# The last layer of a four-layer graph network: whole tiles instead of halves, and a written order

## The chip, the cores and the metric

The kernel runs on one core of one Trainium2 chip. The core has a matrix engine (TensorE, PE in the profile; PEld is its weight load), a vector engine (VectorE, DVE), an activation engine (ScalarE, ACT), GpSimd (POOL) and SyncE (SP), which issues most of the transfers here. Each engine works through its own list of instructions in order and waits on semaphores for the others. Matrix results land in PSUM, eight banks of 512 float32 columns on 128 partitions; everything else is in SBUF. The metric is the device time of one execution in microseconds (us). PSUM is small, and which operations touch it decides how wide they can be in this kernel.

## The reference

Four layers over a graph of 4096 nodes with 64 features; each adds its result to `x` and normalises the rows. The change is in the last one, which works on the Poincare ball:

```python
def _logmap(x, y, c):
    sub = _mobius_add(-x, y, c)
    sub_norm = jnp.maximum(jnp.linalg.norm(sub, axis=-1, keepdims=True), MIN_NORM)
    ...
    arg = jnp.clip(sqrt_c * sub_norm, 0.0, TANH_CLIP)
    return 2.0 / (sqrt_c * lam_x) * jnp.arctanh(arg) * sub / sub_norm
...
deg = jnp.maximum(adj.sum(axis=1, keepdims=True), 1e-08)
w = adj / deg
log_ij = _logmap(x[:, None, :], x[None, :, :], c)
agg = jnp.einsum('ij,ijc->ic', w, log_ij)
transformed = agg @ weight + bias
return _expmap(origin, transformed, c)
```

For every pair of nodes (i, j) a factor is needed that depends on both rows and is the same for (i, j) and (j, i), up to what belongs to one row alone. The kernel computes a number v per pair by a matrix product, then the factor min(ln(v + root), T_MAX) / root, where root is the square root of a floored `v*v - 1` (in scaled units). It multiplies the adjacency by the factor and sums over j with another matrix product. What belongs to one row is multiplied in afterwards.

## The kernel before

The 4096 nodes form 8 groups of 512 (`GW`), in the order of the list `seq`. A tile is a pair of groups (i, j) with j at or after i in that order: 36 tiles, 8 of them on the diagonal. They are taken row by row: row 0 has 8 tiles, row 1 has 7, and so on; the first tile of a row is the diagonal one. A tile is 128 partitions x 4 blocks x 512 columns, that is 2048 columns. Because the factor is symmetric, an off-diagonal tile serves twice: its own adjacency tile (`own`, L1463) is multiplied by the factor, and the mirrored one (`mirrored`, L1469) by the factor turned (transposed) on PE.

The steps of a tile, with halves of two blocks (1024 columns) as the unit n:

- `product` (L1484): PE writes v into a pair of PSUM banks, `ps_v` with two such pairs.
- `square` (L1498): ACT squares v into `w`; `opposite` (L1505): PE adds a small correction product onto the same v.
- `less_one` (L1518): DVE subtracts the one and floors it, in SBUF.
- ACT: Ln of `w` in place (L1718), Exp with scale 0.5 into `rt`, the root (L1719), later Exp with scale -0.5 in place, one over the root (L1745).
- DVE `plus root` (L1743): `rt` becomes v + root; this reads v from PSUM and so frees the bank pair for the `product` of half n + 2.
- ACT: Ln of `rt` (L1754).
- DVE `factor` (L1728): the smaller of `rt` and T_MAX, times `w`, into `f`; then `own products` (L1731): adjacency times `f`.
- `turn` (L1523): PE transposes blocks of `f`, four at a time into one PSUM bank of `ps_p` (two banks, used in turn); DVE multiplies each bank into the mirrored adjacency (L1541), 512 columns per instruction. A diagonal tile turns only one quarter (L1532, L1534), and its second half has only 256 columns per block.
- `gather` (L1544): PE sums the weighted adjacency times the node features into a bank of `ps_a` (two banks): partitions 0 to 63 for row i (L1555), partitions 64 to 127 for the mirrored sum of the tile before (L1567), which in later rows starts from the sum carried in `tb` (L1563). ACT copies the sums to `tb` (L1574, L1578).

One turn of the loop does one half: factor and own products lie two halves behind the roots, the gather one more, the transposes one or two more. PE's matrix products of `product`, `opposite` and `gather` are held in the order of the program by `in_order`; the transposes and all of DVE's and ACT's instructions are ordered by the planner of the language, which places each by priority when its inputs are due. All the tile's steps use the same pools of buffers: four halves of `w`, three of `rt`, two tiles of `f`, three tiles of each adjacency.

Besides the tiles there are small steps in the list `seam`, one taken per turn: the end of the layer before (normalisation of its last groups), the preparation `weights` and `factors`, and for each finished row the five steps of `finals` (L1631), on tiles of at most 128 x 512, with their PSUM results in `ps_p` as well. `right(i)` (L1443) prepares the right-hand sides for a row: two products into `ps_p`, each copied by ACT (L1451). SP issues the loads of 1 MB each, three tiles ahead at the start and then as buffers come free. After the loop the rest of `seam` is worked off: that is the tail in which the last two groups are finished.

The change replaces the loop and the functions around it; `right`, `factors`, `weights`, `finals` and everything ahead of the last layer stay.

Of the kernel before, what the change touches and what calls it, by code (L numbers as in the profile page):

```python
# [62 lines left out]
def gnn4_kernel(  # L63
# [28 lines left out]
    CB = 4  # L92
# [1333 lines left out]
    with tc.tile_pool(name="o3", bufs=1) as op, tc.tile_pool(name="cols3", bufs=3) as cols_p, tc.tile_pool(  # L1426
        name="w3", bufs=4
    ) as wp3, tc.tile_pool(name="el3", bufs=3) as el, tc.tile_pool(name="f3", bufs=2) as fp, tc.tile_pool(
        name="r3", bufs=2
    ) as rp, tc.tile_pool(name="ps_v3", bufs=2, space=PSUM) as ps_v, tc.tile_pool(  # L1430
        name="ps_a3", bufs=2, space=PSUM
    ) as ps_a, tc.tile_pool(name="ps_p3", bufs=2, space=PSUM) as ps_p:
        HB = CB // 2

# [40 lines left out]
        def columns(n):  # L1475

            i, j = tiles[n // 2]
            return slice(2 * P if i == j and n % 2 else 0, GW)

        rights, sums, fs = {}, {}, {}  # L1480
        vs, ws, rts = {}, {}, {}
        NU = 2 * NT

        def product(n):  # L1484

            if n >= NU:
                return
            i, j = tiles[n // 2]
            vs[n] = ps_v.tile([P, HB, GW], F32, name="v_ps")
            cs = columns(n)  # L1490
            for k in range(HB):
                jb = j * CB + (n % 2) * HB + k
                half = slice(jb % 2 * F, jb % 2 * F + F)
                in_order(nc.tensor.matmul(  # L1494
                    vs[n][:, k, cs], lhsT=tr_c[half, jb // 2, :], rhs=rights[i][0][half, cs], start=True, stop=True
                ))

        def square(n):  # L1498
            if n >= NU:
                return  # L1500
            ws[n] = wp3.tile([P, HB, GW], F32, name="w3")
            cs = columns(n)
            nc.scalar.activation(ws[n][:, :, cs], vs[n][:, :, cs], AF.Square)  # L1503

        def opposite(n):  # L1505
            if n >= NU:
                return
            i, j = tiles[n // 2]
            cs = columns(n)
            for k in range(HB):  # L1510
                jb = j * CB + (n % 2) * HB + k
                half = slice(jb % 2 * F, jb % 2 * F + F)
                in_order(nc.tensor.matmul(
                    vs[n][:, k, cs], lhsT=tr_o[half, jb // 2, :], rhs=rights[i][1][half, cs],
                    start=False, stop=True, skip_group_check=True,
                ))

        def less_one(n):  # L1518
            if n < NU:
                w = ws[n][:, :, columns(n)]  # L1520
                nc.vector.tensor_scalar(w, w, -SCALE * SCALE, V_FLOOR * (V_FLOOR + 2.0) * SCALE**2, ALU.add, ALU.max)  # L1521

        def turn(n):  # L1523

            t, h = n
            i, j = tiles[t]
            work = []
            if i == j:
                tp = ps_p.tile([P, GW], F32, name="post", tag="post")
                for k in range(HB):  # L1530
                    for b in range(HB):
                        nc.tensor.transpose(tp[:, cols(HB * k + b)], fs[t][:, b, cols(HB + k)], ident)  # L1532
                to = own[t][:, HB:CB, 0 : HB * P]
                work.append(lambda: nc.vector.tensor_tensor(to, tp.rearrange("p (k i) -> p k i", k=HB), to, ALU.mult))  # L1534
                return work
            for b in (HB * h, HB * h + 1):
                tp = ps_p.tile([P, GW], F32, name="post", tag="post")
                for k in range(CB):
                    nc.tensor.transpose(tp[:, cols(k)], fs[t][:, k, cols(b)], ident)  # L1539
                to = mirrored[t][:, b, :]  # L1540
                work.append(lambda to=to, tp=tp: nc.vector.tensor_tensor(to, tp, to, ALU.mult))  # L1541
            return work

        def gather(t, h, tm):  # L1544

            if t is not None:
                i, j = tiles[t]
                if i == j and h == 0:
                    sums[i] = ps_a.tile([P, GW], F32, name="sums_ps")
                bank = sums[i]  # L1550
            else:
                bank = sums[seq[-1]]
            for k in (HB * h, HB * h + 1):
                if t is not None:
                    in_order(nc.tensor.matmul(  # L1555
                        bank[0:F, :], lhsT=nat_c[:, j * CB + k, :], rhs=own[t][:, k, :],
                        start=(i == j and k == 0), stop=(j == seq[-1] and k == CB - 1), skip_group_check=True,
                    ))
                if tm is not None:
                    above, below = tiles[tm]  # L1560
                    if k == 0 and above != seq[0]:

                        in_order(nc.tensor.matmul(  # L1563
# [3 lines left out]
                    in_order(nc.tensor.matmul(  # L1567
# [3 lines left out]
            work = []  # L1571
            if tm is not None and h:
                to = tb[F:P, gcols(tiles[tm][1])]
                work.append(lambda: nc.scalar.copy(to, bank[F:P, :]))  # L1574
            if t is not None and h and tiles[t][1] == seq[-1]:
                g = tiles[t][0]
                copy = nc.vector.tensor_copy if g == seq[-1] else nc.scalar.copy
                work.append(lambda: copy(tb[0:F, gcols(g)], bank[0:F, :]))  # L1578
                seam.extend(finals(g))
            return work  # L1580
# [113 lines left out]
        turns, late_turns, gathers = {}, {}, {}  # L1694

        for t in range(3):
# [117 lines left out]
```

## Time and profile before

| | us |
|---|---|
| median of three runs | 1417.04 |
| lowest, highest | 1411.5, 1420.06 |
| the profiled execution, its own time | 1415.59 |
| its span, first to last instruction | 1413.9 |
| busy in the span: PE, DVE, ACT | 1308.5, 1052.1, 803.7 |
| first `plus root` (L1743) of the last layer starts at | 982.7 |
| L1743 that opens the last tile starts at | 1375.7 |

The times of steps come from the profiled execution. In a row of groups the columns are the line and the engine, what is written from what, the shape, the count, then the busy time of the group and the mean in nanoseconds of one, then the idle time of the engine just ahead of them and what ended it. A row of the timeline gives start and duration in us. A row of windows gives, for a stretch of time, its length, then busy time and number of instructions of PE, PEld, DVE, ACT and POOL, the clock granted to PE (1.00 is full), the share of the DMA engines and GB/s. Successive instructions of one engine overlap a little, so the step from start to start can be shorter than the duration.

### The profile page before, as it was taken

To read this page: it belongs to the slowest core of one execution; us is meant where nothing else is said; L and a number is where in the kernel's file an instruction comes from. 1 tells how busy PE (TensorE), PEld (TensorE's weight loads), DVE (VectorE), ACT (ScalarE), POOL (GpSimd) and SP (SyncE) were. 2 spreads that over 40 slices of the span, in tenths; PEclk is the share of its full clock that TensorE was granted. 3 is DMA by queue.
4 is the path that set the end of the run, shared out by engine and by line. 5 is a ranking of instruction groups with operands and counts; after the bars stand their busy time and mean duration, and the time that the engine had idled before them with its cause. 6 is when DMAs were issued, how large, how long until landed. Compare 5 with 4: busy or idle time off the path is not lost.

```text
span 1413.9 us, 18980 instructions
## 1 busy us (share of the span) xinstructions
PE 1308.5 (93%) x6766; PEld 604.3 (43%) x6766; DVE 1052.1 (74%) x2012; ACT 803.7 (57%) x1339; POOL 109.8 (8%) x191
## 2 busy tenths in 40 slices
PE   7999999999899998999999999998888899989893
PEld 5655555565344333444444333333333333333331
DVE  6799999898343266788885123446999999999986
ACT  5544443443000115654423675744989999999993
POOL 2110111110122000000110000000000000000000
PEclk9999999999999999999998999998899999999997
DMA  9999999999699999999985555444245454445420
GB/s 326 408 412 411 397 411 409 409 396 398 230 365 388 380 421 378 377 345 331 329 310 191 186 185 179 146 154 175 66 177 189 148 232 150 182 155 202 154 97 12
DMA packets 108191, 382.16 MB, mean 270 GB/s; under 512 B 20276, under 2 KB 20280, under 8 KB 76472
## 3 DMA queue, kind: packets, MB, share of 16 engines
q1 hardware_dynamic: 87096, 296.17, 57.1%
q0 software_dynamic: 12736, 76.29, 13.1%
q10 hardware_dynamic: 8256, 8.39, 1.7%
q8 instruction: 56, 0.92, 0.3%
q14 instruction: 47, 0.39, 0.1%
HBM read 294.05 MB, written 85.20 MB: 268 GB/s over the span
## 4 chain that ended last, share of the span: by engine, by line
PE 59%; ACT 17%; DVE 15%; DMA 4%; issue 3%; ACTq 0%; DVEq 0%; SPq 0%
PE a_ps L1111 8%; PE pass L566 7%; PE w_ps L566 5%; PE tp L657 5%; PE p_ps L1102 5%; PE pass L559 5%; PE cnt_ps L1373 4%; PE acc_ps L1333 4%; DMA raw<-in_adj_dram 3%; ACT w L1718 3%; ACT rt L1719 3%; ACT w L1503 3%; DVE lows L690 2%; ACT rt L1754 2%; DVE dpart L688 2%
## 5 line engine op out<-in xcount | busy, mean ns | idle before, releaser
L664 ACT COPY at<-tp 128x512 f32<-128x512 f32 x248 | 127.8, 598 | 120.8 <-issue 91.1
L1378 ACT ACTIVATE wt<-cnt_ps 128x512 uint16<-128x512 f32 x208 | 115.5, 595 | 72.6 <-PE cnt_ps L1373 67.9
L688 DVE TENSOR_REDUCE dpart<-raw 128x4 f32<-128x2048 f32 x64 | 145.5, 2275 | 5.5 <-DMA raw<-in_adj_dram 5.3
L1555 PE MATMUL sums_ps<-at_d,some 128*64 128x512 f32 x288 | 146.5, 629 | 2.7 <-DVE at_d L1534 1.7
L690 DVE TENSOR_REDUCE lows<-raw 128x1 f32<-128x2048 f32 x64 | 145.5, 2274 | 0.0
L657 PE MATMUL tp<-ident,raw 128*128 128x128 f32 x1024 | 130.8, 281 | 10.1 <-DMA raw<-in_adj_dram 9.0
L657 PEld LDWEIGHTS tp<-ident,raw 128*128 128x128 f32 x1024 | 114.7, 143 | 47.2 <-issue 36.3
L1111 PE MATMUL a_ps<-at,nat_a 128*64 128x512 f32 x512 | 123.3, 609 | 0.0
L1567 PE MATMUL sums_ps<-at_m,some 128*64 128x512 f32 x224 | 110.2, 615 | 0.0
L1494 PE MATMUL v_ps<-rv,tr_a 64*128 64x512 f32 (+1 forms) x288 | 81.7, 645 | 23.2 <-DVE rt L1743 23.2
L566 PE MATMUL pass<-at,cheb_n 128*128 128x512 f32 x224 | 99.2, 601 | 2.4 <-DVE cheb_n L588 1.9
L566 PE MATMUL w_ps<-at,cheb_n 128*128 128x512 f32 x208 | 93.5, 593 | 0.0
L1743 DVE SCALAR_TENSOR_TENSOR rt<-v_ps,rt 128x1024 f32<-128x1024 f32 x72 | 83.5, 1161 | 4.2 <-ACT rt L1719 3.6
L1373 PE MATMUL cnt_ps<-m,follow 128*64 128x512 fp8e4 x480 | 81.7, 391 | 4.6 <-ACT wt L1378 1.5
L1728 DVE SCALAR_TENSOR_TENSOR f<-rt,w 128x1024 f32<-128x1024 f32 x72 | 83.6, 1163 | 1.1 <-ACT rt L1754 1.0
L1731 DVE TENSOR_TENSOR at_d<-at_d,f 128x1024 f32<-128x1024 f32 x72 | 83.7, 1162 | 0.1
L1541 DVE TENSOR_TENSOR at_m<-post,at_m 128x512 f32<-128x512 f32 x112 | 75.4, 686 | 9.5 <-PE post L1539 9.2
L1380 DVE TENSOR_SCALAR wt<-cnt_ps 128x512 uint16<-128x512 f32 x48 | 33.2, 692 | 63.1 <-PE cnt_ps L1373 60.4
L1754 ACT ACTIVATE rt<-rt 128x1024 f32<-128x1024 f32 x72 | 72.1, 1005 | 7.8 <-DVE rt L1743 7.4
L1718 ACT ACTIVATE w<-w 128x1024 f32<-128x1024 f32 x72 | 71.9, 1000 | 5.0 <-DVE w L1521 5.0
L1539 PE MATMUL post<-ident,f 128*128 128x128 f32 x448 | 69.0, 284 | 5.4 <-DVE at_m L1541 4.3
L1745 ACT ACTIVATE w<-w 128x1024 f32<-128x1024 f32 x72 | 72.4, 1006 | 0.6
(396 smaller groups left out, 2222.7 us busy)
## 6 DMA issues: line engine op xcount, KB each, us to landing
at<-adj_t SPq DMA_DIRECT2D x119, 1024.0 KB, 7.9
raw<-in_adj_dram SPq DMA_DIRECT2D x64, 1024.0 KB, 13.5
adj_t<-at POOLq DMA_DIRECT2D x62, 1024.0 KB, 8.1
at_d<-adj_t SPq DMA_DIRECT2D x36, 1024.0 KB, 4.8
at_m<-adj_t SPq DMA_DIRECT2D x28, 1024.0 KB, 6.9
m<-mask_t SPq DMA_DIRECT2D x120, 128.0 KB, 2.8
m<-mask_t SPq DMA_DIRECT2D x60, 256.0 KB, 4.1
mask_t<-mask ACTq DMA_DIRECT2D x28, 256.0 KB, 7.9
```

Of the source, the lines that this page charges most:

```text
L566: in_order(nc.tensor.matmul(ps, lhsT=cheb_n[:, jb, k : k + 2, :], rhs=rhs, start=first, stop=last))
L657: in_order(nc.tensor.transpose(tp[:, cols(b)], raw[:, b, cols(k)], ident))
L664: nc.scalar.copy(at[:, k, :], tp)
L688: in_order(nc.vector.tensor_reduce(dpart[:, g, c, :], raw, AX.X, ALU.add))
L690: in_order(nc.vector.tensor_reduce(lows[:, n : n + 1], raw.rearrange("p b j -> p (b j)"), AX.X, ALU.min))
L1111: in_order(nc.tensor.matmul(ps[q * F : (q + 1) * F, :], lhsT=nat_a[:, c * CB + k, 0:F], rhs=of[q if signed else 0][:, k, :], start=(c == 0 ...
L1373: in_order(nc.tensor.matmul(cnt[a][r * HP : (r + 1) * HP, :], lhsT=follow, rhs=chunks[c][odd][2 * a + r][:, k, :], start=(h == 2 * NB - 1) ...
L1378: in_order(nc.scalar.activation(wt[odd][a], cnt[a], AF.Relu, scale=-128.0))
L1555: in_order(nc.tensor.matmul(bank[0:F, :], lhsT=nat_c[:, j * CB + k, :], rhs=own[t][:, k, :], start=(i == j and k == 0), stop=(j == seq[-1] ...
L1567: in_order(nc.tensor.matmul(bank[F:P, :], lhsT=nat_c[:, above * GB + k, :], rhs=mirrored[tm][:, k, :], start=(k == 0 and above == seq[0]), ...
L1718: nc.scalar.activation(w, w, AF.Ln)
L1754: nc.scalar.activation(rt, rt, AF.Ln, scale=1.0 / SCALE)
```

## The change

The unit of the loop becomes the tile. Operations that touch no PSUM (`less_one`, Ln, both Exp, the second Ln, `factor`, `own products`) are one instruction over 2048 columns for an off-diagonal tile; for a diagonal tile they stay in two parts. `square` and `plus_root` read PSUM and stay in halves. The turned factors go into a pair of banks, and DVE multiplies 1024 columns per instruction. PSUM is divided anew: `ps_v` keeps its four banks, the sums have one bank, the turned factors one pair (`ps_u`), and `right`, `finals` and the like share one bank (`ps_p`). `w` and `rt` have two whole tiles each. Every instruction of the tile's steps on PE, ACT and DVE is tied behind the one before it on its engine by `chained`, so that the order in the program is the order on the engine; the small steps are not tied, and the planner puts them between. Two tiles are loaded ahead instead of three, and two small steps are taken per tile. The new loop, with functions whose bodies changed only from halves to parts left out:

```diff
-        name="w3", bufs=4
-    ) as wp3, tc.tile_pool(name="el3", bufs=3) as el, tc.tile_pool(name="f3", bufs=2) as fp, tc.tile_pool(
+        name="w3", bufs=2
+    ) as wp3, tc.tile_pool(name="el3", bufs=2) as el, tc.tile_pool(name="f3", bufs=2) as fp, tc.tile_pool(
...
-        name="ps_a3", bufs=2, space=PSUM
-    ) as ps_a, tc.tile_pool(name="ps_p3", bufs=2, space=PSUM) as ps_p:
+        name="ps_a3", bufs=1, space=PSUM
+    ) as ps_a, tc.tile_pool(name="ps_u3", bufs=1, space=PSUM) as ps_u, tc.tile_pool(
+        name="ps_p3", bufs=1, space=PSUM
+    ) as ps_p:
...
+        def chained(ins):
+            engine = ins.ins.engine
+            if engine in behind:
+                tc.add_manual_dep(
+                    ins.ins, behind[engine],
+                    mybir.DependencyInfo(mybir.DependencyClass.NoSync, mybir.DependencyReason.DATA),
+                    reason="chained",
+                )
+            behind[engine] = ins.ins.name
+            return ins
...
+        def part(t, h):
+            return slice(h * HB, (h + 1) * HB), slice(2 * P if h and on_diagonal(t) else 0, GW)
+        def parts_of(t):
+            return [part(t, 0), part(t, 1)] if on_diagonal(t) else [(slice(0, CB), slice(0, GW))]
...
+        def less_one(t):
+            for hs, cs in parts_of(t):
+                w = ws[t][:, hs, cs]
+                chained(nc.vector.tensor_scalar(
+                    w, w, -SCALE * SCALE, V_FLOOR * (V_FLOOR + 2.0) * SCALE**2, ALU.add, ALU.max
+                ))
+        def roots(t):
+            rts[t] = el.tile([P, CB, GW], F32, name="rt3")
+            for hs, cs in parts_of(t):
+                w = ws[t][:, hs, cs]
+                chained(nc.scalar.activation(w, w, AF.Ln))
+            for hs, cs in parts_of(t):
+                chained(nc.scalar.activation(rts[t][:, hs, cs], ws[t][:, hs, cs], AF.Exp, scale=0.5))
+            for hs, cs in parts_of(t):
+                w = ws[t][:, hs, cs]
+                chained(nc.scalar.activation(w, w, AF.Exp, scale=-0.5))
+        def plus_root(t, h):
+            hs, cs = part(t, h)
+            rt = rts[t][:, hs, cs]
+            chained(nc.vector.scalar_tensor_tensor(
+                rt, vs.pop((t, h))[:, :, cs], (1.0 + V_FLOOR) * SCALE, rt, ALU.max, ALU.add
+            ))
+        def logs(t):
+            for hs, cs in parts_of(t):
+                rt = rts[t][:, hs, cs]
+                chained(nc.scalar.activation(rt, rt, AF.Ln, scale=1.0 / SCALE))
+        def factor(t):
+            f, rt, w = fp.tile([P, CB, GW], F32, name="f3"), rts.pop(t), ws.pop(t)
+            for hs, cs in parts_of(t):
+                chained(nc.vector.scalar_tensor_tensor(
+                    f[:, hs, cs], rt[:, hs, cs], T_MAX, w[:, hs, cs], ALU.min, ALU.mult
+                ))
+        def own_products(t):
+            for hs, cs in parts_of(t):
+                at = own[t][:, hs, cs]
+                chained(nc.vector.tensor_tensor(at, at, fs[t][:, hs, cs], ALU.mult))
+        def turn(t, h):
+            tp = turned[t, h] = ps_u.tile([P, HB, GW], F32, name="tp")
...
+            for b in range(HB):
+                for k in range(CB):
+                    chained(nc.tensor.transpose(tp[:, b, cols(k)], fs[t][:, k, cols(h * HB + b)], ident))
+        def turned_products(t, h):
+            tp = turned.pop((t, h))
...
+                to = mirrored[t][:, h * HB : (h + 1) * HB, :]
+            chained(nc.vector.tensor_tensor(to, tp, to, ALU.mult))
...
+        for t in range(2):
+            load_own(t)
+            load_mirrored(t)
...
+        for t in range(NT + 2):
+            done, now3 = t - 2, t - 1
+            if done >= 0 and not on_diagonal(done):
+                turn(done, 1)
+            if 0 <= now3 < NT:
+                factor(now3)
+            gather(done, 1)
+            load_own(t + 1)
+            load_mirrored(t)
+            seam_step()
+            if done >= 0 and not on_diagonal(done):
+                turned_products(done, 1)
+            if 0 <= now3 < NT:
+                turn(now3, 0)
+            if t < NT:
+                for h in range(2):
+                    plus_root(t, h)
+                    product(t + 1, h)
+                for h in range(2):
+                    square(t + 1, h)
+                    opposite(t + 1, h)
+            if 0 <= now3 < NT:
+                own_products(now3)
+            if t < NT:
+                logs(t)
+            if t == NT - 3:
+                seam += [ahead_of_last(g) for g in seq[-2:]]
+            seam_step()
+            less_one(t + 1)
+            roots(t + 1)
+            gather(now3, 0)
+            if 0 <= now3 < NT:
+                turned_products(now3, 0)
...
```

## The prediction

> **What bounds the kernel now.** I read the page's busy line first, then the stretch from the first to the last `plus root` operation (L1743) cut by rows of tiles, then the groups with their shapes kept apart, then single stretches of the timeline, then the waits. The busy line is an average over four layers:
>
> ```profile
> PE 1308.5 (93%) x6766; PEld 604.3 (43%) x6766; DVE 1052.1 (74%) x2012; ACT 803.7 (57%) x1339; POOL 109.8 (8%) x191
> ```
>
> The last layer is different. The next view cuts it at the L1743 that opens each row (rows 0 to 6, then the tail); its columns are PE, PEld, DVE, ACT, POOL, clock and DMA:
>
> ```profile
> 982.70:1073.60 90.90, 76.44 (x335) 31.33 (x335) 87.78 (x162) 81.22 (x96) 0.62 (x2) 0.88 0.40 150
> 1073.60:1150.70 77.10, 68.79 (x325) 27.98 (x324) 74.05 (x111) 74.34 (x101) 1.56 (x2) 1.00 0.48 179
> 1150.70:1217.70 67.00, 60.76 (x284) 24.51 (x282) 63.90 (x100) 63.88 (x91) 1.56 (x2) 0.97 0.47 175
> 1217.70:1272.50 54.80, 49.80 (x238) 20.45 (x236) 53.03 (x87) 53.55 (x80) 1.56 (x2) 1.00 0.48 177
> 1272.50:1317.50 45.00, 39.10 (x191) 16.84 (x192) 42.20 (x70) 43.98 (x66) 1.56 (x2) 1.00 0.47 176
> 1317.50:1351.90 34.40, 31.89 (x161) 14.62 (x160) 31.41 (x51) 32.58 (x55) 1.56 (x2) 1.00 0.48 176
> 1351.90:1375.70 23.80, 22.52 (x109) 10.06 (x110) 21.59 (x45) 22.40 (x34) 0.00 (x0) 0.93 0.23 84
> 1375.70:1413.90 38.20, 15.55 (x66) 6.92 (x65) 27.07 (x103) 16.49 (x66) 1.56 (x2) 0.78 0.05 11
> ```
>
> In the first 393 us (seven rows) DVE and ACT are each about 95% busy and PE 89%; DMA, at under half, is hidden. Adding the idle entries of DVE's timeline there gives 17.5 us; the rest, 375.5 us, is 338.2 of tile work and 37.2 of small steps (end of the layer before, `finals`). So DVE and ACT bound the layer together, with PE near behind. A fixed cost saved on one of them alone is worth little.
>
> **Prices.** Shapes kept apart:
>
> ```profile
> L688 DVE TENSOR_REDUCE dpart<-raw 128x4 f32<-128x2048 f32 x64 | 145.5, 2275 | 5.5 <-DMA raw<-in_adj_dram 5.3
> L1743 DVE SCALAR_TENSOR_TENSOR rt<-v_ps,rt 128x1024 f32<-128x1024 f32 x64 | 78.0, 1219 | 4.2 <-ACT rt L1719 3.6
> L1718 ACT ACTIVATE w<-w 128x1024 f32<-128x1024 f32 x64 | 67.1, 1048 | 5.0 <-DVE w L1521 5.0
> L1069 ACT ACTIVATE mask<-at 128x2048 fp8e4<-128x2048 f32 x28 | 52.8, 1908 | 6.0 <-DMA at<-adj_t 3.3 <-DVE first_pos L500 1.1 <-ACT mask L1069 0.9
> L754 DVE TENSOR_SCALAR four<-at 128x2048 fp8e4<-128x2048 f32 x20 | 23.8, 1222 | 4.8 <-DMA at<-adj_t 4.8
> ```
>
> Rows of 128x2048 stand beside 128x1024. On DVE one wide operation takes 2.28 for 2 x 1.22, but successive ones overlap by 0.09 (step 1.13 at 1024), so the step goes from 2 x 1.13 to 2.19: 0.07 saved. The one-source `less one` goes from 2 x 0.60 (L1521) to 1.13: 0.07. Two banks of turned factors in one: 2 x 0.60 (L1541) to 1.13, twice a tile: 0.14. With `factor` and `own products` that is 0.35 per off-diagonal tile, 28 of them: **9.8 us of DVE**. ACT: 2 x 0.95 to 1.81, four operations: 0.36 per tile, **10.1 us**. The 8 diagonal tiles keep halves. But:
>
> ```profile
> 1111.58 1.04 ACT L1718 ACTIVATE w<-w 128x1024 f32<-128x1024 f32 x1
> 1112.65 1.06 ACT L1719 ACTIVATE rt<-w 128x1024 f32<-128x1024 f32 x1
> 1113.61 1.04 ACT L1754 ACTIVATE rt<-rt 128x1024 f32<-128x1024 f32 x1
> ```
>
> L1719 reads what L1718 writes and starts 1.07 after it; L1754, independent, only 0.96 after L1719. In the pinned order Ln, Exp, Exp always follow each other on one tile, so two steps per tile cost 0.12 more: 0.24 of ACT's 0.36 goes back.
>
> **One plain turn of the new order** (off-diagonal tiles around it), from the order in which the changed instructions stand on each engine. Start-to-start steps come from the rows above; a wait costs 0.03 to 0.05 beyond the releaser's end (L1743 of 1099.89 ends 1101.12, its product starts 1101.17). Time 0 is the second `plus root` of tile t.
> - DVE: own products 1.13; less one could start at 3.32; turned products, factor, turned products, two plus roots: 1.13+1.13+2.19+1.13+1.13 later the turn closes at 10.0 without waits.
> - PE and ACT: second product 1.27 to 2.40 (L1494: 1.13), second Square 2.44 to 3.46 (1.02), so less one waits until 3.50, **0.17 idle, closing at 10.2**. Meanwhile logs 3.35, Ln 5.16, Exp 7.09 to 8.99; plus root could start at 9.02 and DVE comes to it at 9.08. ACT's ring is 10.15.
> - PE: from the Square at 3.50: opposite 0.32, gather with the carried sum 2.73, transposes 1.02, gather 1.77, transposes 1.02, product 1.06: the second product at 11.42, needed at 11.47. Ring 10.15.
>
> The three rings lie within 0.1 us. Into a diagonal tile a turn is 9.3 (less DVE work), out of it 9.7 plus 0.3 for two bank copies on ACT ahead of the Squares; one turn later ACT's ring alone decides, 10.15.
>
> **Small steps, now fixed between them.** Per row `finals` puts into ACT's list four v copies (L1657; 0.84) behind the logs: 11.0. In the next turn the Ln of 4 numbers (L1671) stands between the two Squares and waits for a DVE maximum queued behind the 2.19 own product: Square 1.2 late; with 0.5 for a `right` copy the turn is 12.1. Then 1.7 us of small DVE operations plus an ACT Ln and Exp around them: 12.3. Then four L290 outputs (1.34) stand ahead of the logs and wait for a scale queued behind own products (ready near 4.2): 12.4. Rows 1 to 6 by these sums, in the order out of the diagonal, the four with small steps, plain, into the next: 10.0+11.0+12.1+12.3+12.4+10.2+9.3 = 77.3; 67.1 (no plain turn left); 56.0 and 44.4 (outputs fall into the last turn or the next row); 33.7; 22.5. Row 0: in DVE's list tile 1's less one stands behind the previous layer's normalisation: 7.8 us from the first plus root on (two plus roots 1.74, four 128x512 operations at 0.60, a 128x504 one at 0.59, some twenty small ones at 0.07 to 0.10, transposes and their copy 1.3). Then less one, Ln and Exp, 5.0, so 12.8, then 10.7, 11.1, 11.6, 11.8, 11.0, 11.0, 9.3 = 89.3. **Sum 390.3 against 393.0.** The first plus root comes 1.0 later (Squares and Ln of both parts go first: 0.48 + 0.52); the tail is as before, 13.6 against 14.0 from the last plus root to the last sums, and I give the single spare bank (it was two) 1.0. Net: 393.0 - 390.3 - 2.0 = 0.7 gained on the profiled run's 1415.6 (span 1413.9), which lies 1.4 below the median of 1417.0. On the median: **1416**.
>
> Costed at nothing: loads. Two tiles instead of three are fetched ahead; a freed buffer is refilled one turn (10 us) before use, and landings take 4.8 and 6.9. Without that cover one landing, 7 us, once at the start. A cold clock in row 0 (0.88 granted already) could add 0 to 3; I take 0, because DVE waits there for DVE. One sum bank instead of two: its copies end before the next row's first gather, 0; bound, seven waits of 0.6.
>
> A rule against the change is in the Trainium skill, Perfetto Trace Analysis, section Matmuls: groups should rotate through different banks, so that draining one overlaps the next. The transposes lose that rotation. L1539 waited 16.6 us in 34 waits for L1541 with two banks. By the rule, 56 pairs each released 0.62 later would cost up to 35 us; in the turn above the second set is released at 9.2, PE reaches it at 9.35, and the cost is nothing.
>
> **Rivals.**
> 1. *Faster, 1392 (chance 0.17).* The waits I charge to `finals` find cover. For it: DVE's 17.5 us of idle is spread thin, and DVE falls to 365.7. Keeping only 0.17 in 15 plain turns, 368 against 393 is 25 less. Against: pinned lists cannot step around a late operation.
> 2. *Slower, 1434 (0.29).* The small steps' hops between ACT and DVE stand behind a whole-tile step of 2.19 or 1.93, where halves made it 1.13 or 1.07. I charged three a row. Five more in six rows at 0.6 each add 18. It decides from about four more (14 us). For it: all rings close within 0.1, so any wait is paid on all three engines. Against: most remaining hops have half a turn of slack.
> 3. *The saving is not there:* wide operations cost twice the narrow. Then 7 us more, inside the forecast's own range.
>
> The forecast has 0.54. A change of 1%, 14 us, is about what a measurement of this kernel can tell from none. Faster by more: 0.17; within: 0.53; slower: 0.30, with the tail of the forecast. Range 1394 to 1440: rival 1 lies just under its lower end, rival 2 and a missed landing are inside.
>
> **What would show it.** Factor at 128x2048 near 2.28 and Ln near 1.90; DVE busy about 10 less; plain turns of 10.2 between L1565 pairs; less one waiting 0.17 for the Square; ACT waiting over 0.5 for a DVE maximum and for a scale, once a row; row 0 near 89. Rows 2 us shorter each would speak for rival 1; PE, DVE and ACT each idle over 8% for rival 2. A long wait on a load or a spare bank would make the whole sum wrong.

## The result, and the profile after

The changed kernel takes 1433.6 us (median of 4, 1429.6 to 1435.6) against 1416.9 for the kernel before: ratio 1.0129, 95% interval 1.0108 to 1.0151, so slower by 1.3%. Forecast was 1416, no change; rival 2 of the prediction had put the slower case at 1434. The profiled execution after took 1429.6, 14.0 more than the one before.

Below, lines are those of the changed kernel: L1514 product, L1524 Square, L1544 less one, L1555 Ln, L1557 Exp 0.5, L1560 Exp -0.5, L1565 plus root, L1572 logs, L1578 factor, L1585 own products, L1605 turned products, L1466 `right`'s copies; of `finals`, L1678 the weighing of x on PE, L1719 its product on DVE, L1727 the squares of v on ACT. The page of the changed kernel, busy time and instructions of each engine:

```profile
PE 1302.8 (91%) x6766; PEld 610.6 (43%) x6766; DVE 1046.8 (73%) x1872; ACT 794.1 (56%) x1227; POOL 104.7 (7%) x191
```

DVE is 5.3 less busy than before and ACT 9.6. The cut by rows, at the L1565 that opens each row (rows 0 to 6, then the tail; columns as in the prediction's table):

```profile
982.10:1077.86 95.76, 75.72 (x339) 33.66 (x339) 88.75 (x132) 80.62 (x69) 0.62 (x2) 0.91 0.36 142
1077.86:1156.76 78.90, 67.20 (x324) 28.60 (x324) 72.80 (x81) 72.39 (x78) 0.65 (x2) 0.98 0.46 175
1156.76:1226.36 69.60, 58.38 (x284) 24.90 (x282) 62.67 (x75) 62.59 (x71) 0.65 (x2) 1.00 0.44 168
1226.36:1283.88 57.52, 48.98 (x238) 21.05 (x236) 52.18 (x68) 51.23 (x62) 0.65 (x2) 1.00 0.44 167
1283.88:1330.30 46.42, 41.58 (x209) 18.84 (x208) 41.11 (x52) 43.81 (x56) 0.65 (x2) 1.00 0.43 160
1330.30:1365.63 35.33, 28.37 (x137) 12.37 (x135) 30.61 (x42) 30.53 (x45) 0.65 (x2) 1.00 0.46 180
1365.63:1388.09 22.46, 21.57 (x111) 10.38 (x112) 20.20 (x40) 20.58 (x29) 0.00 (x0) 1.00 0.29 100
1388.09:1427.90 39.81, 15.69 (x69) 7.89 (x67) 27.02 (x100) 16.54 (x66) 0.65 (x2) 0.74 0.05 10
```

The seven rows take 406.0 (1388.09 - 982.10) instead of 393.0; the tail 39.8 instead of 38.2. In row 1 DVE is busy 92% (72.80 of 78.90) where it was 96%. Adding the idle entries of the timelines over the rows gives 34.8 for DVE (17.5 before) and 41.4 for ACT (18.0 before): the work got less, the waiting got more. The groups, shapes kept apart, show that each wide operation has the price that was forecast:

```profile
L1578 DVE SCALAR_TENSOR_TENSOR f<-rt,w 128x2048 f32<-128x2048 f32 x28 | 63.9, 2282 | 4.3 <-ACT rt L1572 4.2
L1557 ACT ACTIVATE rt<-w 128x2048 f32<-128x2048 f32 x28 | 53.6, 1914 | 0.7
L1544 DVE TENSOR_SCALAR w<-w 128x2048 f32<-128x2048 f32 x28 | 34.2, 1223 | 13.8 <-ACT w L1524 13.6
L1565 DVE SCALAR_TENSOR_TENSOR rt<-v_ps,rt 128x1024 f32<-128x1024 f32 x64 | 76.2, 1216 | 8.0 <-ACT rt L1557 7.9
```

DVE's largest new wait stands in the third line: the one less one of a tile waits 13.6 in all for the second Square of that tile; its two halves had waited 3.6. ACT's largest is the Square that waits for its product on PE, 20.4 in all where it was 3.2 (3.98 of it once, in row 0, shown further down). The lines, two of before and then the changed kernel's Square:

```profile
L1521 DVE TENSOR_SCALAR w<-w 128x1024 f32<-128x1024 f32 x64 | 44.0, 687 | 3.6 <-ACT w L1503 3.6
L1503 ACT ACTIVATE w<-v_ps 128x1024 f32<-128x1024 f32 x64 | 65.0, 1016 | 3.7 <-PE v_ps L1494 3.2
L1524 ACT ACTIVATE w<-v_ps 128x1024 f32<-128x1024 f32 x64 | 64.2, 1022 | 22.0 <-PE v_ps L1514 20.4 <-PE post L1658 0.8
```

Turns, from the start of a tile's first L1565 to the next tile's, tell where the time lies. In row 2, with row 1's plain turn (rows 1 and 3 repeat the others within 0.1, but for a first of 9.62 and a second of 12.05 in row 1 and a last of 10.29 in row 3):

| turn | forecast | after |
|---|---|---|
| out of the diagonal tile | 10.0 | 9.86 |
| second | 11.0 | 12.78 |
| third | 12.1 | 12.35 |
| fourth | 12.3 | 12.25 |
| fifth | 12.4 | 12.48 |
| plain | 10.2 | 10.26 |
| into the next diagonal tile | 9.3 | 9.88 |

### The profile page after: what moved, and what is told of

It reads as the page before. It is cut to its first block, busy times and chain, and to the rows that moved or that the text cites. A ratio compares the mean times of both kernels' runs of the same rounds, so it can differ in the third digit from the quotient of the medians.

```text
span 1427.9 us, 18723 instructions
## 1 busy us (share of the span) xinstructions
PE 1302.8 (91%) x6766; PEld 610.6 (43%) x6766; DVE 1046.8 (73%) x1872; ACT 794.1 (56%) x1227; POOL 104.7 (7%) x191
## 4 chain that ended last, share of the span: by engine, by line
PE 65%; DVE 14%; ACT 13%; DMA 5%; issue 3%; ACTq 0%; DVEq 0%; SPq 0%
PE a_ps L1111 8%; PE pass L566 7%; PE tp L657 7%; PE w_ps L566 6%; PE p_ps L1102 5%; PE pass L559 4%; PE cnt_ps L1373 4%; DMA raw<-in_adj_dram 4%; PE acc_ps L1333 4%; PE h_ps L559 3%; PE sums_ps L1617 3%; DVE at_d L1585 3%; DVE rt L1565 2%; ACT wt L1378 2%; ACT rt L1557 2%
## 5 line engine op out<-in xcount | busy, mean ns | idle before, releaser
L1617 PE MATMUL sums_ps<-at_d,some 128*64 128x512 f32 x288 | 139.9, 612 | 5.0 <-DVE at_d L1585 5.0
L1629 PE MATMUL sums_ps<-at_m,some 128*64 128x512 f32 x224 | 106.0, 599 | 0.0
L1514 PE MATMUL v_ps<-rv,tr_a 64*128 64x512 f32 (+1 forms) x288 | 79.6, 635 | 16.4 <-DVE rt L1565 15.4
L1565 DVE SCALAR_TENSOR_TENSOR rt<-v_ps,rt 128x1024 f32<-128x1024 f32 x72 | 81.1, 1156 | 8.0 <-ACT rt L1557 7.9
L1578 DVE SCALAR_TENSOR_TENSOR f<-rt,w 128x2048 f32<-128x2048 f32 (+2 forms) x44 | 78.4, 1798 | 4.5 <-ACT rt L1572 4.4
L1524 ACT ACTIVATE w<-v_ps 128x1024 f32<-128x1024 f32 x72 | 68.2, 974 | 23.6 <-PE v_ps L1514 22.0
L1585 DVE TENSOR_TENSOR at_d<-at_d,f 128x2048 f32<-128x2048 f32 (+2 forms) x44 | 78.5, 1796 | 0.0
L1597 PE MATMUL tp<-ident,f 128*128 128x128 f32 x448 | 62.1, 282 | 17.2 <-DVE at_m L1605 16.1
L1597 PEld LDWEIGHTS tp<-ident,f 128*128 128x128 f32 x448 | 49.3, 143 | 58.8 <-DVE at_m L1605 48.5
L1605 DVE TENSOR_TENSOR at_m<-tp,at_m 128x1024 f32<-128x1024 f32 x56 | 68.1, 1216 | 2.1 <-PE tp L1597 1.8
L1555 ACT ACTIVATE w<-w 128x2048 f32<-128x2048 f32 (+2 forms) x44 | 66.3, 1522 | 5.6 <-DVE w L1544 5.5
```

The costliest lines, as they stand in the source:

```text
L1565: chained(nc.vector.scalar_tensor_tensor(rt, vs.pop((t, h))[:, :, cs], (1.0 + V_FLOOR) * SCALE, rt, ALU.max, ALU.add))
L1585: chained(nc.vector.tensor_tensor(at, at, fs[t][:, hs, cs], ALU.mult))
L1597: chained(nc.tensor.transpose(tp[:, b, cols(k)], fs[t][:, k, cols(h * HB + b)], ident))
L1617: chained(nc.tensor.matmul(bank[0:F, :], lhsT=nat_c[:, j * CB + k, :], rhs=own[t][:, k, :], start=(i == j and k == 0), stop=(j == seq[-1] ...
```

## The experiments

"Rows" is, from the profile, the time from the first plus root to that of the last tile, as above (406.0 for the changed kernel, 393.0 for before); the ratio is to the kernel before, on the same chip.

| run | time, us | ratio, 95% interval | rows |
|---|---|---|---|
| changed kernel | 1433.6 | 1.0129 (1.0108 to 1.0151) | 406.0 |
| bare_before | 1396.0 | 0.9859 (0.9829 to 0.9888) | 375.7 |
| bare_after | 1392.8 | 0.9849 (0.9820 to 0.9878) | 371.5 |
| bare_halves | 1388.9 | 0.9836 (0.9819 to 0.9852) | 367.7 |
| singles | 1432.0 | 1.0123 (1.0095 to 1.0151) | 406.4 |
| three_banks | 1434.3 | 1.0143 (1.0113 to 1.0174) | 407.9 |
| early_x | 1425.5 | 1.0077 (1.0060 to 1.0094) | 401.3 |
| no_hop | 1431.9 | 1.0126 (1.0109 to 1.0143) | 405.1 |
| halves | 1419.0 | 1.0034 (1.0016 to 1.0051) | 397.5 |
| half_less | 1427.8 | 1.0109 (1.0084 to 1.0134) | 402.5 |
| half_dve | 1429.8 | 1.0104 (1.0073 to 1.0135) | 404.0 |
| half_act | 1424.2 | 1.0068 (1.0045 to 1.0091) | 396.8 |
| pe_pinned | 1480.0 | 1.0467 (1.0449 to 1.0484) | 458 |
| halves_pe_pinned | 1420.2 | 1.0039 (1.0023 to 1.0054) | 398.4 |
| halves_early | 1412.8 | 1.0008 (0.9996 to 1.0020) | 391.3 |
| half_less_pool | 1421.5 | 1.0069 (1.0050 to 1.0087) | 397.8 |
| out_pool | 1408.9 | 0.9958 (0.9943 to 0.9973) | 385.3 |
| out_sq_pool | 1404.6 | 0.9937 (0.9918 to 0.9955) | 383.2 |
| whole_out_sq | 1417.9 | 1.0027 (1.0015 to 1.0039) | 394.4 |

**Without the small steps.** In both kernels `finals` of the first six groups became a copy and the store:

```diff
+            if not late:
+                return [nothing, nothing, nothing, nothing, nothing, bare]
             return [nothing, first, second, third, fourth, fifth]
```

> The kernel before, with the small steps of finals left out for the first six groups: each stores its rows of x unchanged instead (one GpSimd copy and the same store), so those rows of the output lack the last layer's result; the last two groups and all 36 tiles are as they were. Theory 1 (the loop itself is as forecast, the small steps in pinned places cost the time): rows 1 to 6 fall from 302 us to about 281 (plain turns of 10.6, the step that the unburdened turns of before show), so about 1396. Theory 2 (whole tiles and fixed lists lengthen every turn): the same here; it differs in the next run.

> The changed kernel with the same steps left out in the same way (the first six groups' rows of the output are x unchanged). Theory 1: every turn falls to the 9.87, 10.26 and 9.86 that unburdened turns show now, rows 1 to 6 go from 310 us to about 273, the time to about 1397, level with or up to 5 us below the same cut of the kernel before although row 0 still loses 5. Theory 2: the difference of 16.7 us between the two kernels stays above 12 when the small steps are gone.

Measured: 1396.0 and 1392.8. The 16.7 between the kernels are gone; the intervals of the two ratios overlap. So the small steps of `finals` cost 20.6 in the kernel before and 40.8 in the changed one: more than the whole loss. Theory 1 is right on the totals. One part of it is not: row 0, which has no `finals`, keeps its length (96.5), and before's bare turns are not all near 10.6: those of row 1 lie between 9.0 and 13.5.

**The banks.** `singles` gives each turned factor a bank and a product of its own; `three_banks` draws these two banks and the one for small matmuls from one set:

```diff
-            tp = turned[t, h] = ps_u.tile([P, HB, GW], F32, name="tp")
+            tp = turned[t, h] = [ps_u.tile([P, 1, GW], F32, name="tp") for b in range(HB)]
...
+                for b in range(HB):
+                    to = mirrored[t][:, h * HB + b, :]
+                    chained(nc.vector.tensor_tensor(to, tp[b][:, 0, :], to, ALU.mult))
```

> The changed kernel with turned factors in single banks, two of them, each multiplied by a 512-wide product of its own, as before the change; the one bank for small matmuls stays one. Theory 1: 0.14 us of DVE more per off-diagonal tile, 28 of them: +4, so 1437, row 0 and the small steps' turns otherwise the same. Theory 3 (transposes and products that share a pair of banks stop each other; single banks rotate): plain turns below 10.2 and a time of 1428 or less.

> As the kernel with single banks, and the two banks of turned factors and the one of small matmuls are taken from one set of three in turn. Theory 4 (the one bank for small matmuls: in row 0 the sums of the layer before wait on PE for ScalarE's copy behind a whole-tile Exp, with tile 1's product behind them; in the second turn of a row the weighing of x waits for the v copies): row 0 falls from 95.8 us to about 92, the second turns by about 1 us in five rows, so 8 to 9 less than with single banks alone, about 1428. Theory 1 without a share of the banks: the same time as single banks alone, 1437.

Measured: the time of the changed kernel in both. With single banks a plain turn is 10.38 instead of 10.26, the 0.14 of DVE; the turns with small steps in rows 1 to 3 keep their length within 0.4 either way, and the 4 us expected do not come. No rotation gain either: theory 3 falls. With three banks the turns 0 and 1 of row 0 take 23.2 instead of 27.7, as theory 4 said, but the sums of the layer before now stand ahead of the first tile's product, the first plus root comes 4.5 later, and turns 2 to 4 are longer: row 0 is 95.9, as in the changed kernel. The second turns do not get shorter (11.98 in row 1, 12.84 in rows 2 and 3), so the bank was not their cause.

**The weighing of x.** Done for every group ahead of its row's end, and copied:

```diff
+            if t < NT and tiles[t][1] == seq[-1] and tiles[t][0] not in seq[-2:]:
+                ahead_of_last(tiles[t][0])(ps_p)
```

> The changed kernel, with the weighing of x (four matmuls) of the first six groups done one turn before the end of their row and copied out by ScalarE, as the last two groups have it. Theory 1 (in the second turn after a diagonal tile the product by al waits on DVE for these matmuls, which stand on PE behind two whole gathers, and the squares of v then hold ScalarE): that turn falls from 12.1 to 12.8 to about 11.0 in five rows, -8, and the copy costs 0.36 in six, +2; so about 1427. Theory 5 (the turn is long by the amount of small work in it, whichever wait ends last): the second turn stays above 12 and the time within 3 us of 1433.

In the timeline of the changed kernel, PE reaches L1678 behind two whole gathers; DVE waits 1.86 for it, and ACT, whose list has a square of v ahead of the Exp, waits 1.75 for DVE:

```profile
1176.93 1.10 PE L1678 MATMUL post<-wh_x,tr_a 128*128 128x64 f32 x8
1178.07 0.42 DVE L1719 TENSOR_TENSOR agg<-post,al 128x256 f32<-128x256 f32 x1 [1.86 <-PE post L1678]
1179.51 0.26 ACT L1727 ACTIVATE sqv<-v 128x64 f32<-128x64 f32 x1 [1.75 <-DVE v L1721]
1179.77 1.89 ACT L1560 ACTIVATE w<-w 128x2048 f32<-128x2048 f32 x1
```

In `early_x` the same two operations (one line further down) start without a wait:

```profile
1181.54 0.42 DVE L1720 TENSOR_TENSOR agg<-xw,al 128x256 f32<-128x256 f32 x1
1182.99 0.26 ACT L1728 ACTIVATE sqv<-v 128x64 f32<-128x64 f32 x1
```

Measured: second turns of 11.2 to 11.3 in rows 1 to 3 (1.6 less in rows 2 and 3, 0.7 in row 1) and 1425.5, as theory 1 had it. The second turn of row 4 keeps its 12.21.

**One hop less.**

```diff
-                nc.vector.tensor_scalar_max(n, n, MIN_NORM * MIN_NORM)
-                nc.scalar.activation(n, n, AF.Ln)
+                nc.scalar.activation(n, n, AF.Ln, bias=floor)
```

> The changed kernel, with the floor under the squared norm given to ScalarE's Ln as a bias (added) in place of DVE's maximum: one hop from ScalarE to DVE and back less in each finals. Theory 1 (the Ln of four numbers between the two Squares waits for a maximum that is queued behind the 2.28 us own product): the second Square comes 1.2 earlier, the turn falls from 12.35 to about 11.2 in six rows, so -6, about 1427. Theory 5: the turn keeps its length, since the next small step or wait takes the place: within 2 us of 1433.

Measured: no gain; the third turn of rows 1 to 3 is 12.4 to 13.0, the fourth 0.4 shorter at most. With the wait gone, the Ln and both small Exps go between the two Squares, with `right`'s copy; the second Square comes 5.50 into the turn instead of 5.21. Theory 5 holds here: what decides is how much stands between the Squares.

**Halves again, in the same fixed lists.**

```diff
-            return [part(t, 0), part(t, 1)] if on_diagonal(t) else [(slice(0, CB), slice(0, GW))]
+            return [part(t, 0), part(t, 1)]
```

> The changed kernel, its fixed lists and its banks, with every whole-tile operation again as two halves, one after the other (turned factors stay in pairs of banks). Rival 2 of the prediction (hops stand behind a whole-tile step of 2.2 or 1.9; halves make it 1.1): plain turns of 10.5 to 10.7 instead of 10.26, the turns with small steps down from 12.3 to about 11.5, in all about 1422. Theory 1 (the places in the lists count, not the size of the operations, since both halves stand ahead of the small step alike): every turn 0.2 to 0.4 longer, about 1442.

> The kernel with halves, with the small steps of finals left out for the first six groups (their rows of the output are x unchanged). It prices the whole tile alone, against the same cut of the changed kernel at 1392.8: by the prediction's sum (0.35 us of DVE, 0.12 of ScalarE per off-diagonal tile) 0.2 to 0.35 more in each of some 27 turns, 1398 to 1402. If whole tiles save nothing on the path: 1393 or less.

Measured: 1419.0, about three quarters of the loss back (1.0034 against 1.0129). By rows, what stays lies in row 0: 95.4 with halves, 95.8 with whole tiles, 90.8 before; rows 1 to 6 take 302.1 with halves, 302.1 before and 310.2 with whole tiles. So that part belongs to the rest of the change (order, buffers, loads, banks), of which only the banks were tried by themselves. Nor do halves end ACT's wait for the product: 17.4 in the seven rows, 19.6 with whole tiles. And without the small steps it is 1388.9 against 1392.8 with whole tiles (the intervals of the two ratios overlap). So whole tiles show no saving on the path even without `finals`. A plain turn is 10.25 with them and 10.27 with halves; in row 2 their second turn takes 10.37 against 9.36, the third 10.25 against 10.56, the last 10.30 against 10.01. Rows 1 to 6 of the two bare kernels, as windows (whole tiles first, then halves):

```profile
1076.89:1351.96 275.07, 246.54 (x1184) 102.86 (x1184) 256.45 (x203) 261.27 (x226) 0.00 (x0) 1.00 0.49 184
```

```profile
1079.20:1350.09 270.89, 247.48 (x1192) 103.25 (x1192) 257.96 (x265) 265.43 (x311) 0.00 (x0) 1.00 0.48 187
```

ACT works 4.2 less with whole tiles and idles 8.3 more (13.8 against 5.5). The steps tell one reason; the changed kernel, then `halves`:

```profile
1212.61 1.89 ACT L1555 ACTIVATE w<-w 128x2048 f32<-128x2048 f32 x1
1214.54 1.91 ACT L1557 ACTIVATE rt<-w 128x2048 f32<-128x2048 f32 x1
1216.48 1.92 ACT L1560 ACTIVATE w<-w 128x2048 f32<-128x2048 f32 x1
```

```profile
1187.42 1.99 ACT L1557 ACTIVATE rt<-w 128x1024 f32<-128x1024 f32 x2
1189.31 1.05 ACT L1560 ACTIVATE w<-w 128x1024 f32<-128x1024 f32 x1
```

A whole Exp starts 1.93 after the Ln that feeds it, or 1.94 after the Exp that reads what it overwrites (1.93 to 1.96 over the 34 such pairs of the rows that have no other wait), 0.03 to 0.04 after the end; two halves of an Exp take 1.89, and with halves no operation stands next to the one that feeds it: neighbours overlap.

**Which engine's halves.** One or several operations alone went back to `(part(t, 0), part(t, 1))`: less one; DVE's three; ACT's four.

> The changed kernel with one operation alone back in halves: less one, so that its first half can start at the end of the first Square; all others stay whole, the lists and banks as they are. Theory 7 (a small step on ScalarE delays the second Square, and the one wide less one then holds DVE for both; its wait for a Square was 13.6 us in 13 waits with whole tiles and 5.1 in 9 with halves): most of the 14.6 that the kernel with halves gave back comes with this operation alone, less 0.07 for each of 28 tiles: the time 1421 to 1424, DVE's wait for a Square about 5. Rival 2 as the prediction put it (small hops stand behind the wide own products, factor, logs and roots): these are all still whole, so 1431 or more.

> The changed kernel with DVE's three whole-tile operations (less one, own products, factor) in halves and ScalarE's four whole. Halves on both engines gave back 14.6, less one alone 5.8. Theory 2a (what counts is where a small DVE operation can stand between the halves: the maximum, the five of th, the statistics): about 1421. Theory 2b (ScalarE's whole Ln and Exps hold the small Ln and Exp of finals, and each waits for its predecessor's whole tile): no better than less one alone, 1427.

> The changed kernel with ScalarE's four whole-tile operations (Ln, two Exps, logs) in halves and DVE's three whole. Theory 2a: less than 4 of the 14.6 come back, 1430 or more. Theory 2b: 9 or more, 1424 or less. ScalarE's steps by the traces so far: 1.95 for a whole Exp behind the Ln that feeds it, 1.89 for two halves, so 0.05 less in halves too.

Measured by rows: less one alone gives back 3.5 of 406, DVE's three 2.0, ACT's four 9.2, both engines' 8.6; by ratios 0.2, 0.25, 0.6 and 0.95%. The intervals of the two DVE runs reach to that of the changed kernel, so their share stays open; theory 7 falls as the main cause (in `half_less` the wait for the Square does go from 13.6 to 5.5, but in rows 1 to 3 the third to fifth turns get only 0.2 to 1.0 shorter and the second no shorter). Theory 2b holds in the main: most of what halves give back comes with ScalarE's operations. In the third turn of row 2, which falls from 12.35 to 10.80, the changed kernel had the lines above (the square of v ahead of L1560, waiting 1.75), then a copy and a Ln between the Squares, and so:

```profile
1185.67 1.23 DVE L1544 TENSOR_SCALAR w<-w 128x2048 f32<-128x2048 f32 x1 [1.65 <-ACT w L1524]
```

In `half_act`, whose list has a gap every 0.95 instead of every 1.94, the planner put the same small operations behind the two halves of Exp -0.5, and those waits are gone or short although less one is still whole:

```profile
1177.37 2.01 ACT L1560 ACTIVATE w<-w 128x1024 f32<-128x1024 f32 x2
1180.05 0.26 ACT L1727 ACTIVATE sqv<-v 128x64 f32<-128x64 f32 x1
1183.59 1.23 DVE L1544 TENSOR_SCALAR w<-w 128x2048 f32<-128x2048 f32 x1 [0.16 <-ACT w L1524]
```

**The fixed lists.** The order was written out for PE alone:

```diff
-            if engine in behind:
+            if engine in behind and engine == mybir.EngineType.PE:
```

> The changed kernel with the order written out for PE alone; on DVE and ScalarE the planner sets it by its costs and due times. Theory 1 (fixed lists cannot step around a late small step): the turns with small steps fall from 12.3 to 11.5 or less, plain turns stay within 0.3 of 10.26, the time about 1415. Theory 6 (the planner does no better with whole tiles: with one operation per stage it has little to put between): turns of 12 and more remain, the time at 1430 or above.

> The kernel with halves (1419.0), its order written out for PE alone, DVE and ScalarE left to the planner. With whole tiles that cost 46. If the planner's order is bad because one operation per stage leaves it nothing to put between: with halves within 10 of 1419. If the operations as the program now states them (all three roots of a tile next to each other) do not suit its costs whatever their size: 1445 or more.

Measured: 1480.0 with whole tiles, 1420.2 with halves. So the lists are no cause of the loss: with halves they change nothing, and with whole tiles the planner by itself does far worse. Theory 1's reason ("fixed lists cannot step around a late small step") falls; the size decides, and with whole tiles the lists save most of what it would cost (59.8 between the two sizes without them, 14.6 with them).

**Towards a faster kernel.** The early weighing with halves, then small work moved to GpSimd:

> Halves, and the weighing of x one turn before the row's end. Theory 1: the two effects lie in different turns and add: 1419.0 - 8 = 1411, against 1414 to 1417 for the kernel before. If halves had taken the same wait already: 1417 or more.

> Less one in halves, the weighing of x early, and of finals in the first six groups four additions and products of 128x256 and the scaling of the output on GpSimd in place of DVE and ScalarE. Theory 1 (DVE and ScalarE close every turn, so small work taken off both shortens it where it opens no new wait): DVE loses 4 x 0.36, ScalarE 4 x 0.24 and the wait for a scale of 0.8, in six rows: about 10 below the sum of the two other edits (1421 - 8 = 1413), so 1403. Rival (GpSimd's 0.73 a piece instead of 0.42, and the hops to it, put a new wait into ScalarE's list): 1413 or more.

> Halves, the weighing of x early, and the scaling of the output (L290 of the changed kernel, four ScalarE operations, 1.34) as two GpSimd operations of 128x256 for the first six groups. The wait of ScalarE for the scale and 1.34 of its list go, six times: the turn in which they stand 1.0 shorter, 1412.8 - 6 = 1407. Rival (that turn is set by DVE's small operations, ScalarE waits in any case): 1411 to 1413.

> As the last, and the squares of v (four ScalarE operations with a running sum, 0.96, between the two Squares) as one GpSimd product of 128x256 (0.73) and one DVE sum (0.35) for the first six groups. Theory 1: the second Square no longer stands behind them, that turn 0.6 shorter in six rows, 3 to 4 below the last. Rival: the hop to GpSimd and back makes the maximum and the Ln of the norm late: no gain or a loss.

```diff
+            if pool:
+                nc.gpsimd.tensor_tensor(dst, y, over_rows(r), ALU.mult)
+                nc.gpsimd.tensor_tensor(dst, dst, over_rows(s), ALU.add)
+                return
...
+                    nc.gpsimd.tensor_tensor(sq, v, v, ALU.mult)
+                    nc.vector.tensor_reduce(n, sq, AX.X, ALU.add)
```

The early weighing gains less with halves than the 8 us expected: 0.26% by ratios, against 0.52% with whole tiles, the intervals of `halves` and `halves_early` just overlapping. The output on GpSimd gains 0.50%, clear of noise. The squares add 0.21%, 3 to 4 us as expected, but the intervals of `out_pool` and `out_sq_pool` overlap. `half_less_pool` missed its 1403 by 18: there the additions on GpSimd stand in a chain that DVE waits for (its statistics wait 5.7 for v in five waits, and third and fourth turns of rows 1 to 3 are 12.7 to 13.1). Of the work moved, the output, whose result is wanted late, is the part that shows its worth. `out_sq_pool` beats both kernels: 0.9937 of before.

> The fastest kernel so far (weighing of x early, squares of v and scaling of the output on GpSimd; 1404.6) with the whole tiles of the changed kernel in place of halves. With all small steps the two sizes differ by 14.6, with none by 4.0. Theory 2b (whole ScalarE operations are dear where small ScalarE operations stand in their list): with fewer of these in the list the difference lies between, 6 to 11, so 1411 to 1416. If whole tiles are dear for another reason: 14 or more, 1419 and above.

Measured: 13.3 more than `out_sq_pool`, above the range that theory 2b gave. Counting the small operations of `finals` was not enough; where the planner puts `right`'s copies counts too. Third turn of row 2 in `whole_out_sq` (13.17; its lines are four further down): the copy L1470 stands ahead of Exp -0.5 and waits for PE, and less one pays once more:

```profile
1178.17 0.59 ACT L1470 COPY rv<-post 128x512 f32<-128x512 f32 x1 [1.23 <-PE post L1467]
1178.65 1.91 ACT L1564 ACTIVATE w<-w 128x2048 f32<-128x2048 f32 x1
1183.64 1.23 DVE L1548 TENSOR_SCALAR w<-w 128x2048 f32<-128x2048 f32 x1 [1.59 <-ACT w L1528]
```

The same turn of `out_sq_pool` (10.90): the copy stands between the Squares and waits for nothing, and half a less one fits beside it:

```profile
1174.82 1.02 ACT L1528 ACTIVATE w<-v_ps 128x1024 f32<-128x1024 f32 x1
1175.74 0.58 ACT L1470 COPY rv<-post 128x512 f32<-128x512 f32 x1
1176.46 0.68 DVE L1548 TENSOR_SCALAR w<-w 128x1024 f32<-128x1024 f32 x1
```

This is a part of the answer only. The same copies stand in `bare_after`, where those into `rv` wait for nothing (3.4 in all in `whole_out_sq`) and whole tiles cost 4.0; and by rows the third turns of rows 1 to 3 hold 5.2 of the 11.2 between the two kernels. Where the rest comes from is not shown.

## Why the prediction was wrong

1. **Prices: right.** 2.28, 1.91 and 1.22 stand in the groups; the dependent step on ACT was put at 1.81 + 0.12 and measured 1.93 to 1.94. The sum made of them was half right: "9.8 us of DVE" and "10.1 us of ACT" show as 5.3 and 9.6 of busy time, and against `bare_halves` no saving shows on the path. A part of the reason is in the steps: on ACT two halves that do not follow their feeder take 1.89, so a whole operation is dearer wherever it depends on its neighbour; I had compared it with before's halves, of which some were dependent too.
2. **The plain turn: right.** 10.2 forecast, 10.26 measured, 10.24 to 10.25 bare. Into a diagonal tile I had 9.3 for 9.87: 0.6 too little, in rows 0 to 2.
3. **"With small steps 11.0 (four v copies)": the step that failed first.** 12.05 to 12.9 measured, 1.0 to 1.9 more in each of rows 1 to 5. The sum has no term for the weighing of x on PE, which put it at nothing without a reason; it stands behind two whole gathers, DVE waits 1.86 for it, and a square of v then holds ACT for 1.75. `early_x` takes that out, and in rows 1 to 3 the turn is 11.2 to 11.3.
4. **"12.1, 12.3, 12.4": sizes right (12.35, 12.25, 12.48), the reason given for the first not.** I charged 1.2 to the Ln that waits for DVE's maximum. `no_hop` takes the maximum away and gains nothing; `half_act` keeps it and gains 1.3 to 1.5. By these two runs what holds the turn is how much the planner puts ahead of Exp -0.5 and between the Squares.
5. **Row 0, "12.8, then 10.7": failed by 0.6 and 3.6.** The timeline of the changed kernel:

```profile
993.56 1.91 ACT L1557 ACTIVATE rt<-w 128x2048 f32<-128x2048 f32 x1
995.38 0.35 ACT L1219 CAST some<-post 128x256 bf16<-128x256 f32 x1
995.79 3.68 PE L1281 MATMUL post<-wd,sums 128*128 128x64 f32 x16 [1.90 <-ACT some L1219]
1001.52 1.02 ACT L1524 ACTIVATE w<-v_ps 128x1024 f32<-128x1024 f32 x1 [3.98 <-PE v_ps L1514]
```

   The sums of the layer before (L1281) need the one spare bank, which a cast on ACT frees only behind a whole Exp; tile 1's product stands behind them on PE. The clock granted to PE is 0.50 from 993 to 1003 (before: 0.50 from 982.7 to 993, 0.75 in the next ten), and at it the product's eight passes take 3.79 where most later ones, at 1.00, take 2.26. I had put "the single spare bank" at 1.0 in the tail and nothing here, and the cold clock at 0. `three_banks` takes 4.5 off turns 0 and 1, `halves` 5.1, but the row as a whole stays at 95.9 and 95.4; so what makes row 0 6.5 longer than forecast stays open in the main.
6. **The rest**: the start came 0.6 earlier than before instead of 1.0 later and the tail cost 1.6 instead of 1.0, both within what they vary from run to run. Row by row, forecast and after: 89.3 and 95.8, 77.3 and 78.9, 67.1 and 69.6, 56.0 and 57.5, 44.4 and 46.4, 33.7 and 35.3, 22.5 and 22.5. The sum is 390.3 and 406.0: of the 15.7 too few, 6.5 lie in row 0 and 9.2 in rows 1 to 6.
7. **Rival 2: right in kind, its figure partly by luck.** Small hops behind whole-tile steps cost 18 by its sum, all in six rows; those rows miss the forecast by 9.2, and row 0, of which it says nothing, brings the total near its 1434. In kind it holds: with small steps whole tiles cost 14.6 more than halves, without them 4.0, and its sign is there (over the seven rows the table above leaves DVE idle for 9.3%, ACT for 10.9% and PE for 15.8%; before it was 4.8, 5.4 and 11.1%). It was given 0.29 and not 0.54 because I took most of the hops to have half a turn of slack; that was argued from one turn of my own making. On ACT the slack was not there: its four operations alone in halves take 0.6% off. Its words for DVE's 2.19 step are not shown.
8. **Rival 1** needed cover for `finals`' waits: there was none. **The bank rule** that I weighed and costed at nothing: `singles` agrees, within the interval.

That `halves` gains 14.6 by medians and 8.6 by the profiled rows comes from the executions that were profiled: the changed kernel's is the fastest of its four, 4.0 under the median, that of `halves` lies 2.2 over its own, and the two differ by 8.4. What stays open is row 0, the 13.3 of `whole_out_sq`, and the start and the tail of the profiled runs, which vary over all of them from 980.4 to 988.0 and from 35.0 to 40.7.

## What to carry to other kernels

When two or three engines close the same ring, an operation twice as wide need not save its small fixed cost; here no saving showed on the path even without `finals`, and with it the wide form cost 14.6. Price the small steps at the grain of the large ones around them, on the engine where they wait for another engine's result. Ahead of making operations wider, take the small ones out of the list (earlier, or to an idle engine if their result is wanted late), and look at start-to-start steps, not at busy time. A version without the small steps, in both forms, tells in two runs which of the two matters.

## What was not expected of the hardware

On ACT two independent 1024-column operations take 1.89 from start to start, one of 2048 columns 1.81 with an independent follower (L1572 to L1555 at 1210.80 and 1212.61) but 1.93 to 1.94 ahead of one that reads its result or overwrites its input. So the wide form is the slower one in a chain. GpSimd took 0.61 for five of the six products of 128x256 in `out_sq_pool` and 0.99 for the sixth; the twelve steps of the output's scaling took from 0.61 to 1.13 there and from 0.61 to 2.53 beside whole tiles in `whole_out_sq`.
